# Gated cross-attention block: a tile's scores issued in two pieces, with a new plan of due times

## The chip, the core and the metric
The kernel runs on one core of a Trainium2 chip. The metric is device microseconds of one execution. Engines are written as the profile writes them: PE (TensorE matmuls), PEld (its weight loads), DVE (VectorE), ACT (ScalarE), POOL (GpSimd) and SP (SyncE, which issues the loads).

## What is computed
All is float32. For 8 batch entries of 256 tokens and width 128 there is first one gated cross-attention with 16 heads of 8, then six layers, each of windowed attention (16 heads of 64, windows of 32 queries that see their own and the previous window's 64 keys) and a gated feed-forward part.

```python
x = x + tanh(g_xattn) * xattn(layernorm(x), ctx, ctx)          # 16 heads of 8
y = layernorm(x)
for i in range(6):
    # attn: q, k, v = shift(y) @ Wqkv[i]; q, k are scaled to length 1, by q_scale, k_scale
    # and rotated; softmax(8 * q k^T) over 64 keys a window, masked; then @ v, then @ Wo[i]
    y = attn(shift(y)) + y
    # ffn: layernorm, a, gate = split(@ W1 + b1); (a * gelu(gate)) @ W2 + b2, inner width 341
    y = ffn(shift(y)) + y
out = x + tanh(g_ffn) * y
```

## The kernel before, in words
**Sequences and pieces.** Six layers of eight batch entries make 48 sequences, numbered k = layer * 8 + entry. A sequence's work is cut into small functions, the pieces. `at(k, piece, fn)` gives each piece the time k * 5 + PLAN[piece], in units of which a sequence has 5; all pieces of the program are then sorted by that time (the last lines of `tile_gated_block`, L928 to L930) and issued in that order. So PLAN alone sets the order in each engine's queue. PLAN spans 22 units, so that pieces of some four or five sequences are interleaved: "@-2" below means a piece of the sequence two before the current one. The framework adds the semaphore waits that the order needs. A tile is given to a new user once its last reader in program order has been issued; the new user waits for that reader.

**Pieces of a sequence** (t is one of two tiles of 128 tokens; each name with the line of its instruction):
- proj (L532, tile pj, PE): queries and keys, chunk c of 4 (k of tile 0, q of tile 0, k of tile 1, q of tile 1) in two halves. sq (L540, ACT) squares them into sq, which has one buffer; rot (L548, DVE) multiplies by the rotation tables; ss (L557, DVE) sums the squares; radd (L563, POOL) adds the halves of the rotation; norms (L571, ACT), ninv (L576 to L579, DVE) and nrm (L586, POOL) scale to length 1.
- pqt (L596, PE): 16 transposes of a chunk into the PSUM tile pqt; qe (L604, ACT): two copies of it into qT or kT.
- vp (L611, PE) and ve (L619, ACT): the values.
- sc0 and sc1 (L633, tile pss, PE): the scores of a tile, 8 pairs of heads * 2 * 4 windows, 64 calls, each of which is two weight loads and two matmuls of 64x64 in the profile, so 128 and 128.
- mx (L649, DVE): mask and maximum, group g = (tile, parity), half i: four heads (pairs 4i to 4i+3). ex (L659, ACT): exponentials and their sums of the same four. rs (L668, DVE) and div (L674, POOL): a group's division.
- pt (L692, tiles ppt, PE): 64 transposes of the probabilities of a tile; pe (L701 and L703, DVE, and ACT for (0, 0)) and co (L709, DVE) copy them to prT.
- at, aw (L730, tile po, PE) for two halves c: values by probabilities, with av (L741, DVE) between them and oe (L744, ACT) behind; wo (L753, PE) the output projection, oadd (L516 and L517, DVE).
- ftr (L766, tile px, PE) transposes back; fst (L182 to L185, DVE) the statistics; frs (L189, POOL) the power; fno (L193, tile xn, DVE); fba (L782, tile pxt, PE) transposes again; faf (L787, tile xnT, DVE); fga and fva (L802, tiles s and pa, PE) the up-projection, gate half first; fge (L809, ACT) gelu; fgt (L815, DVE); fdo (L826, tile pw, PE) the down-projection; fad.

**The cross stage**, one run for each batch entry (X0 to X7), begins ahead of the sequences: xt (L226) transposes, xqk (L234) projects, four units xs (L287, tile pssx, scores) with three maxima xm each (L297, DVE), xvp and xve (L252, L258) the values, xnt and xnc (L304 on PE, L308 on DVE, tile nm) turn the maxima, four units xp (L317, tile pssT) with exponentials xe (L328, ACT), xa and xo (L335, L343), then xu, xd, xw, xc, xwo (L348 to L378), xx, xst2, xr2, xn2, xt2, xsp (L381 to L401). Entry b's run is shifted by CROSS_SHIFT[b].

**PSUM.** Pool ps_p (2 buffers) holds pj, pv, px; ps_s (2 buffers of two banks) holds pqt, pss, po, one part of ppt, and s; ps_m (2 buffers) the others.

**Order of the issue of a sequence in the steady part**, from PLAN:

```
PE    proj01 fva@-4 proj00 at0@-3 sc1@-2 aw0@-3 fdo@-4 proj11 at1@-3 proj10 aw1@-3 pqt2@-1
      vp00@-1 wo0@-3 proj20 proj21 wo1@-3 pqt0@-1 pqt1@-1 proj31 ftr@-3 pt0@-2 sc0@-1 pqt3@-1
      vp10@-2 fba@-3 proj30 vp11@-1 fga@-3 pt1@-2 vp01@-2
DVE   ... rot20 rot21 oadd@-3 ss2 fst@-3 rot31 pe02@-2 fno@-3 mx01@-1 mx10@-1 pe01@-2 faf@-3
      rs2@-2 mx11@-1 mx00@-1 ss3 rot30 pe11@-2 pe12@-2 co@-2 pe10@-2
ACT   sq01 norms@-1 sq00 ex10@-2 oe0@-3 ex11@-2 sq11 ex00@-2 sq10 oe1@-3 ex31@-2 ve00@-1
      ex30@-2 sq20 qe21@-1 sq21 qe20@-1 ex20@-2 qe01@-1 qe00@-1 qe10@-1 qe11@-1 sq31 pe00@-2
      ex21@-2 qe31@-1 qe30@-1 ve10@-2 sq30 ex01@-1 ve11@-1 fge@-3 ve01@-2
```

**Order of a cross cycle** (X2 with X1 behind it and X0 ending):

```
PE    ... xa3.X1 xs2.X2 xa2.X1 xs1.X2 xu0.X1 xs0.X2 xu1.X1 xs3.X2 xt2.X0 xw.X1 xvp.X2 xnt.X2
      xt.X3 xp1.X2 xwo.X1 xqk.X3 xp0.X2 ...
```

Of the kernel before, what the change touches and what calls it, by code (L numbers as in the profile page):

```python
# [10 lines left out]
F32 = mybir.dt.float32  # L11
# [6 lines left out]
P = 128  # L18
# [7 lines left out]
DEPTH, HEADS, DH, WIN = 6, 16, 64, 32  # L26
KEYS = 2 * WIN
INNER = HEADS * DH
NPAIR = HEADS // 2
# [5 lines left out]


PLAN = {
    "proj01": 0.0, "sq01": 0.117, "rot01": 0.228, "proj00": 0.236, "sq00": 0.273, "rot00": 0.393,
    "ss0": 0.402, "proj11": 0.419, "sq11": 0.907, "rot11": 0.994, "proj10": 1.19, "sq10": 1.393,
    "rot10": 1.525, "ss1": 1.637, "radd1": 1.837, "proj20": 1.868, "sq20": 2.141, "rot20": 2.287,  # L40
    "proj21": 2.345, "sq21": 2.456, "rot21": 2.806, "ss2": 3.078, "radd0": 3.11, "proj31": 3.269,
    "sq31": 3.608, "rot31": 3.615, "proj30": 3.952, "sq30": 4.191, "radd2": 4.58, "ss3": 4.594,
    "rot30": 4.73, "norms": 5.141, "ninv": 5.35, "radd3": 5.599, "nrm2": 5.783, "nrm0": 5.955,
    "nrm3": 6.257, "pqt2": 6.415, "vp00": 6.565, "ve00": 6.664, "nrm1": 6.997, "qe21": 7.448,
    "qe20": 7.701, "pqt0": 7.799, "qe01": 7.896, "qe00": 7.932, "pqt1": 8.239, "qe10": 8.288,
    "qe11": 8.292, "sc0": 8.693, "pqt3": 8.78, "mx01": 8.907, "mx10": 8.927, "qe31": 9.004,
    "qe30": 9.09, "mx11": 9.28, "vp11": 9.287, "mx00": 9.458, "ex01": 9.514, "ve11": 9.589,
    "sc1": 10.324, "ex10": 10.374, "mx21": 10.605, "mx30": 10.609, "mx31": 10.696, "ex11": 10.807,
    "mx20": 10.859, "ex00": 11.32, "ex31": 11.408, "rs0": 11.679, "rs1": 11.757, "ex30": 11.855,
    "div1": 12.001, "rs3": 12.206, "div0": 12.294, "ex20": 12.875, "pt0": 13.461, "pe02": 13.622,  # L50
    "pe00": 13.707, "ex21": 13.784, "vp10": 13.787, "pe01": 14.102, "ve10": 14.121,
    "div3": 14.146, "rs2": 14.264, "div2": 14.336, "pt1": 14.54, "vp01": 14.624, "pe11": 14.821,
    "pe12": 14.867, "co": 14.868, "ve01": 14.935, "pe10": 14.949, "at0": 15.268, "av0": 15.27,
    "aw0": 15.36, "oe0": 15.434, "at1": 15.442, "av1": 15.705, "aw1": 16.363, "oe1": 16.404,
    "wo0": 16.588, "wo1": 17.415, "oadd": 17.94, "ftr": 18.346, "fst": 18.466, "frs": 18.529,
    "fno": 18.644, "fba": 18.801, "faf": 19.161, "fga": 19.492, "fge": 19.912, "fva": 20.011,
    "fgt": 20.187, "fdo": 20.398, "fad": 21.554, "zt": 21.653, "zg": 21.768,
    "xld": -22.25, "xst": -21.971, "xrs": -21.307, "xno": -20.581, "xt": -20.222, "xte": -20.092,
    "xqk": -19.736, "xqe": -19.735, "xke": -19.676, "xs2": -18.806, "xm21": -18.472,
    "xm22": -18.442, "xm20": -18.393, "xs1": -18.085, "xm11": -17.986, "xm12": -17.982,  # L60
    "xm10": -17.865, "xs0": -17.758, "xm01": -17.411, "xb": -17.355, "xm02": -17.348,
    "xs3": -17.326, "xm00": -17.273, "xm30": -17.198, "xvp": -17.075, "xm32": -17.038,
    "xm31": -17.012, "xve": -16.975, "xnt": -16.951, "xnc": -16.928, "xp1": -16.726,
    "xe12": -16.402, "xe11": -16.398, "xe10": -16.387, "xp0": -16.101, "xa1": -16.052,
    "xe02": -15.992, "xe01": -15.973, "xe00": -15.915, "xo1": -15.91, "xp3": -15.851,
    "xa0": -15.831, "xe31": -15.811, "xe32": -15.807, "xo0": -15.797, "xe30": -15.793,
    "xp2": -15.612, "xa3": -15.596, "xe21": -15.584, "xe22": -15.472, "xo3": -15.415,
    "xe20": -15.213, "xa2": -14.816, "xo2": -14.731, "xu0": -14.462, "xd0": -14.387,
    "xu1": -14.088, "xd1": -13.915, "xw": -13.791, "xc": -13.71, "xwo": -13.217, "xx": -13.195,
    "xst2": -12.619, "xr2": -11.475, "xn2": -10.599, "xt2": -10.456, "xsp": -10.398,  # L70
}

CROSS_SHIFT = [0.000, -1.653, -3.255, -4.780, -6.339, -7.886, -8.007, -9.173]
LOAD_FIRST, LOAD_AFTER, LOAD_AFTER_CROSS = -18.898, 21.60, -19.52

P_ON_SCALAR = {(0, 0)}

# [2 lines left out]
def tile_gated_block(ctx: ExitStack, tc: tile.TileContext, a: dict, out: bass.AP):  # L80
# [5 lines left out]
    small = ctx.enter_context(tc.tile_pool(name="small", bufs=4))  # L86
# [5 lines left out]
    ps_s = ctx.enter_context(tc.tile_pool(name="ps_s", bufs=2, space=PSUM))  # L92
# [10 lines left out]
    def at(k, piece, fn, *args):  # L103
        time = PLAN[piece] if isinstance(piece, str) else piece
        pieces.append((k * SLOTS + time, len(pieces), fn, args))

    def once(c_, key, pool, shape, tag, **kw):

        if key not in c_:
            c_[key] = pool.tile(shape, F32, tag=tag, name=tag, **kw)  # L110
        return c_[key]
# [86 lines left out]
    def cross(b):  # L198
# [203 lines left out]

        kx = b + CROSS_SHIFT[b] / SLOTS
        for n, fn in (
# [116 lines left out]
    def sequence(k, l, b, weights):  # L521

        c_ = {}
# [95 lines left out]
            nc.scalar.copy(v[:, t, half * 512 : (half + 1) * 512], c_.pop(("pv", t, half)))  # L619


        def scores(t):
            for x in ("sums", "rs"):
                c_[x, t] = small.tile([P, HEADS], F32, tag=x, name=x)
            pss = ps_s.tile([P, 2, NPAIR, KEYS], F32, tag="s", name="pss")
            c_["pss", t] = pss
            for c in range(NPAIR):
                for par in range(2):
                    rows = slice(par * DH, (par + 1) * DH)
                    for n in range(BLOCKS):  # L630
                        o = t * P + n * WIN
                        k0 = max(o - WIN, 0)
                        nc.tensor.matmul(  # L633
                            pss[n * WIN : (n + 1) * WIN, par, c, :],
                            c_["qT"][rows, c, o : o + WIN],
                            c_["kT"][rows, c, k0 : k0 + KEYS],
                            start=True, stop=True,
                        )
# [208 lines left out]
                at(k, f"vp{t}{half}", v_project, t, half)  # L847
                at(k, f"ve{t}{half}", v_evacuate, t, half)
        for t in range(NT):
            at(k, f"sc{t}", scores, t)  # L850
            at(k, f"pt{t}", p_transpose, t)
            for x in range(3):
                at(k, f"pe{t}{x}", p_evacuate, t, x)
# [67 lines left out]
    for l in range(DEPTH):  # L921
        at(l * B, tables, scale_tables, l)
        if l:

            at((l - 1) * B if l > 1 else B - 1, LOAD_AFTER if l > 1 else LOAD_AFTER_CROSS, load, l)
        for b in range(B):
            sequence(l * B + b, l, b, layers)
# [61 lines left out]
```

## Time and profile before
| what | value |
|---|---|
| median of three runs | 1841.89 us (1837.06 to 1842.74) |
| the profiled execution | 1843.98 us |
| its span, first to last instruction | 1842.2 us |
| mean granted TensorE clock | 0.974 |
| busy: PE, DVE, ACT, POOL | 1726.1, 1523.1, 1495.4, 1095.2 us |
| chain that ended last, by engine | PE 86%, DVE 6%, issue 5%, ACT 3%, POOL 1% |

A busy PE is a TensorE with matmuls in flight; the ends of matmuls are modelled, so times below are taken from one start to the next. The chain follows back from the last instruction what released each step; "issue" is time in which an engine waited for nothing that the profile shows. In the timeline, a row merges neighbouring instructions of a kind, and the bracket at its end is the engine's idle time ahead of it.

### The profile page before, as it was taken

To read this page: it belongs to the slowest core of one execution; us is meant where nothing else is said; L and a number is where in the kernel's file an instruction comes from. 1 tells how busy PE (TensorE), PEld (TensorE's weight loads), DVE (VectorE), ACT (ScalarE), POOL (GpSimd) and SP (SyncE) were. 2 spreads that over 40 slices of the span, in tenths; PEclk is the share of its full clock that TensorE was granted. 3 is DMA by queue.
4 is the path that set the end of the run, shared out by engine and by line. 5 is a ranking of instruction groups with operands and counts; after the bars stand their busy time and mean duration, and the time that the engine had idled before them with its cause. 6 is when DMAs were issued, how large, how long until landed. Compare 5 with 4: busy or idle time off the path is not lost.

```text
span 1842.2 us, 78203 instructions
## 1 busy us (share of the span) xinstructions
PE 1726.1 (94%) x32948; PEld 1151.3 (62%) x32948; DVE 1523.1 (83%) x5314; ACT 1495.4 (81%) x4692; POOL 1095.2 (59%) x716
## 2 busy tenths in 40 slices
PE   7999788999999999999999999999999999999987
PEld 4555454666666666666666666666666666666664
DVE  3544666888989999898999889999989999999864
ACT  2343357898989989898999989999989999998983
POOL 3111345665766667666676767767666777666741
PEclk9999989999999999999999999999999999999998
DMA  3000002000001000011000010000110000000000
GB/s 92 7 13 7 7 1 66 3 3 3 3 3 61 10 3 2 3 37 33 3 3 3 3 49 21 3 3 3 37 33 3 3 3 3 3 6 6 8 6 10
DMA packets 34717, 26.33 MB, mean 14 GB/s; under 512 B 16058, under 2 KB 31294, under 8 KB 34366
## 3 DMA queue, kind: packets, MB, share of 16 engines
q1 hardware_dynamic: 33214, 21.20, 3.9%
q8 instruction: 259, 4.24, 1.0%
q14 instruction: 92, 0.75, 0.1%
q10 hardware_dynamic: 1152, 0.14, 0.0%
HBM read 20.28 MB, written 1.05 MB: 12 GB/s over the span
## 4 chain that ended last, share of the span: by engine, by line
PE 86%; DVE 6%; issue 5%; ACT 3%; POOL 1%; POOLq 0%; ACTq 0%; DVEq 0%
PE pj L532 19%; PE pv L611 11%; PE m L753 9%; PE po L730 8%; PE pss L633 8%; PE pqt L596 6%; PE ppt L692 6%; PE s L802 5%; PE pssT L317 4%; PE pw L826 4%; DVE x_max L297 3%; PE pa L802 2%; PE pox L335 2%; ACT pr L328 1%; DVE ur L548 1%
## 5 line engine op out<-in xcount | busy, mean ns | idle before, releaser
L563 POOL TENSOR_TENSOR u<-ur 128x1024 f32<-128x1024 f32 x192 | 454.3, 2366 | 120.8 <-DVE ur L548 89.1
L659 ACT ACTIVATE pr<-pr,nmax 128x64 f32<-128x64 f32 x1536 | 515.2, 342 | 0.6
L586 POOL TENSOR_TENSOR u<-u,rn 128x1024 f32<-128x1024 f32 x192 | 361.3, 1903 | 192.0 <-DVE rn L579 192.0
L532 PE MATMUL pj<-w_qkv,st 128*128 128x512 f32 x768 | 404.4, 618 | 7.7 <-ACT x_big L343 2.3
L674 POOL TENSOR_TENSOR pr<-pr,rs 128x512 f32<-128x512 f32 x192 | 198.3, 1044 | 196.8 <-DVE rs L668 196.8
L659 ACT ACTIVATION_READ_ACCUMULATOR pr<-pr,nmax 128x1 f32 x1536 | 296.9, 193 | 0.0
L540 ACT ACTIVATE sq<-pj 128x512 f32<-128x512 f32 x384 | 230.3, 600 | 62.9 <-PE pj L532 52.2
L548 DVE TENSOR_TENSOR ur<-pj,rotk 128x1024 f32<-128x1024 f32 x192 | 227.1, 1202 | 44.9 <-ACT sq L540 43.8
L649 DVE CUSTOM_DVE_ANT_0 pr<-pss,mask 128x64 f32<-128x64 f32 x1536 | 233.6, 218 | 20.0 <-PE pss L633 19.4
L548 DVE TENSOR_TENSOR ur<-pj,rotq 128x1024 f32<-128x1024 f32 x192 | 230.1, 1218 | 14.0 <-ACT sq L540 13.8
L557 DVE TENSOR_REDUCE squares<-sq 128x16 f32<-128x1024 f32 x192 | 233.2, 1215 | 6.5 <-ACT sq L540 4.4
L611 PE MATMUL pv<-w_qkv,st 128*128 128x512 f32 x384 | 223.1, 664 | 0.8 <-DVE ur L548 0.8
L730 PEld LDWEIGHTS po<-prT,v 64*64 64x64 f32 x6144 | 134.3, 133 | 121.3 <-issue 38.7
L633 PE MATMUL pss<-kT,qT 64*32 64x64 f32 x12288 | 152.4, 227 | 46.8 <-issue 46.8
L532 PEld LDWEIGHTS pj<-w_qkv,st 128*128 128x128 f32 x768 | 134.7, 193 | 76.8 <-issue 38.8
L753 PEld LDWEIGHTS m<-oT,w_o 128*128 128x128 f32 x768 | 145.5, 190 | 58.9 <-issue 43.3
L753 PE MATMUL m<-oT,w_o 128*128 128x256 f32 x768 | 181.9, 380 | 0.0
L730 PE MATMUL po<-prT,v 64*64 64x96 f32 (+1 forms) x6144 | 171.5, 243 | 10.3 <-issue 6.2
L633 PEld LDWEIGHTS pss<-kT,qT 64*32 64x32 f32 x12288 | 130.5, 105 | 61.4 <-issue 53.4
L189 POOL TENSOR_TENSOR rstd<-rstd,half_neg 128x2 f32<-128x2 f32 x64 | 44.9, 702 | 176.0 <-DVE rstd L185 176.0
L604 ACT COPY qT<-pqt 128x512 f32<-128x512 f32 x192 | 104.3, 605 | 53.5 <-PE pqt L596 53.5
L701 DVE COPY prT<-ppt 128x512 f32<-128x512 f32 x192 | 127.3, 684 | 10.1 <-PE ppt L692 6.8
(116 smaller groups left out, 2879.0 us busy)
## 6 DMA issues: line engine op xcount, KB each, us to landing
w_qkv<-in_L_ffn_Wqkv SPq DMA_DIRECT2D x18, 512.0 KB, 5.6
w_o<-in_L_ffn_Wo SPq DMA_DIRECT2D x6, 512.0 KB, 4.1
w<-in_L_ffn_W SPq DMA_DIRECT2D x6, 341.0 KB, 2.8
xin<-in_x SPq DMA_DIRECT2D x8, 128.0 KB, 2.9
cin<-in_ctx SPq DMA_DIRECT2D x8, 128.0 KB, 2.1
out<-res SPq DMA_DIRECT2D x8, 128.0 KB, 1.8
w<-in_L_ffn_W SPq DMA_DIRECT2D x12, 64.0 KB, 3.4
rotq<-in_c_cos_q SPq DMA_DIRECT2D x6, 64.0 KB, 3.9
```

Of the source, the lines that this page charges most:

```text
L532: nc.tensor.matmul(pj, st[b][:, t * P : (t + 1) * P], w["qkv"][:, o : o + 512], start=True, stop=True,)
L540: nc.scalar.activation(sq[:, hs, :], c_["pj", c, half], AF.Square)
L548: nc.vector.tensor_tensor(ur[:, :, half * 512 : (half + 1) * 512].rearrange("p x (h d) -> p x h d", d=DH), pj.unsqueeze(1).to_broadcast([P ...
L557: nc.vector.tensor_reduce(squares[k % 2][:, t, i, :, 0], c_.pop(("sq", c)), AX.X, ALU.add)
L563: nc.gpsimd.tensor_tensor(u.rearrange("p h (two d) -> p h two d", two=2), ur[:, 0], ur[:, 1, :, ::-1, :], ALU.add,)
L586: nc.gpsimd.tensor_tensor(u, u, rn, ALU.mult)
L611: nc.tensor.matmul(pj, st[b][:, t * P : (t + 1) * P], w["qkv"][:, o : o + 512], start=True, stop=True,)
L633: nc.tensor.matmul(pss[n * WIN : (n + 1) * WIN, par, c, :], c_["qT"][rows, c, o : o + WIN], c_["kT"][rows, c, k0 : k0 + KEYS], start=True, ...
L649: nc.vector.tensor_tensor_reduce(probabilities(t)[:, par * NPAIR + c, :], c_["pss", t][:, par, c, :], mask[:, t, :], -1.0, 3e38, ALU.add, ...
L659: nc.scalar.activation(pr[:, col, :], pr[:, col, :], AF.Exp, bias=c_.pop(("nmax", g, c)), scale=-1.0, accum_out=c_["sums", t][:, col : col ...
L730: nc.tensor.matmul(po[par * DH : (par + 1) * DH, x, i, q0:q1], v[rows, t, h * DH : (h + 1) * DH], prT[rows, column[h], 64 * half : 64 * ha ...
L753: nc.tensor.matmul(pm, weights[l]["o"][:, c, :], oT[:, c, :], start=(first and c == 4 * half), stop=(not first and c == 4 * half + 3),)
```

## The change
`scores` takes a second argument: piece i issues the pairs 4i to 4i+3. Both pieces write the same PSUM tile, and the instructions are the same.

```diff
-        def scores(t):
+        def scores(t, i):
             for x in ("sums", "rs"):
-                c_[x, t] = small.tile([P, HEADS], F32, tag=x, name=x)
-            pss = ps_s.tile([P, 2, NPAIR, KEYS], F32, tag="s", name="pss")
-            c_["pss", t] = pss
-            for c in range(NPAIR):
+                once(c_, (x, t), small, [P, HEADS], x)
+            pss = once(c_, ("pss", t), ps_s, [P, 2, NPAIR, KEYS], "s")
+            for c in range(4 * i, 4 * i + 4):
...
         for t in range(NT):
-            at(k, f"sc{t}", scores, t)
+            for i in range(2):
+                at(k, f"sc{t}{i}", scores, t, i)
```

PLAN has a new time for every piece, CROSS_SHIFT and the times of the weight loads too:

```diff
-    "qe11": 8.292, "sc0": 8.693, "pqt3": 8.78, "mx01": 8.907, "mx10": 8.927, "qe31": 9.004,
+    "qe11": 7.79232, "qe10": 7.79416, "qe01": 7.86086, "qe00": 7.86486, "sc01": 8.08564,
+    "sc00": 8.08586, "mx01": 8.33529, "mx00": 8.575, "mx10": 8.73408, "ex01": 8.84437,
+    "mx11": 9.0029, "pqt3": 9.30081, "qe30": 9.30558, "vp11": 9.34495, "qe31": 9.3858,
...
-    "sc1": 10.324, "ex10": 10.374, "mx21": 10.605, "mx30": 10.609, "mx31": 10.696, "ex11": 10.807,
+    "ve11": 9.41571, "ex00": 10.61127, "sc10": 10.70937, "sc11": 10.76862, "mx20": 11.07451,
...
-CROSS_SHIFT = [0.000, -1.653, -3.255, -4.780, -6.339, -7.886, -8.007, -9.173]
-LOAD_FIRST, LOAD_AFTER, LOAD_AFTER_CROSS = -18.898, 21.60, -19.52
+CROSS_SHIFT = [0.0000000, -1.4843600, -2.9659400, -4.3950700, -5.7931900, -7.2641000, -8.5043100, -8.5733000]
+LOAD_FIRST, LOAD_AFTER, LOAD_AFTER_CROSS = -19.7106000, 21.63, -19.98
```

The order that follows from it, for the same stretches as above:

```
PE    proj01 fva@-4 proj00 at0@-3 sc10@-2 sc11@-2 aw0@-3 proj11 fdo@-4 at1@-3 proj10 aw1@-3
      pqt2@-1 vp00@-1 wo0@-3 proj21 proj20 wo1@-3 pqt1@-1 pqt0@-1 proj31 ftr@-3 pt0@-2
      sc01@-1 sc00@-1 vp10@-2 fba@-3 proj30 pqt3@-1 vp11@-1 fga@-3 pt1@-2 vp01@-2
DVE   ... rot21 rot20 oadd@-3 ss2 rs3@-2 fst@-3 rot31 pe01@-2 fno@-3 mx01@-1 mx00@-1 mx10@-1
      mx11@-1 faf@-3 rs2@-2 pe02@-2 rot30 co@-2 ss3 pe12@-2 pe11@-2 pe10@-2
ACT   norms@-1 sq01 sq00 ex00@-2 oe0@-3 sq11 ex10@-2 ex11@-2 sq10 oe1@-3 ve00@-1 ex30@-2
      qe21@-1 sq21 qe20@-1 sq20 ex31@-2 qe11@-1 qe10@-1 qe01@-1 qe00@-1 sq31 ex20@-2 pe00@-2
      ex21@-2 ve10@-2 ex01@-1 sq30 qe30@-1 qe31@-1 ve11@-1 fge@-3 ve01@-2
PE    ... xa3.X1 xt2.X0 xs2.X2 xa2.X1 xvp.X2 xs1.X2 xu0.X1 xs0.X2 xu1.X1 xs3.X2 xt.X3 xw.X1
      xwo.X1 xnt.X2 xp1.X2 xqk.X3 xp0.X2 ...
```

On DVE the cross cycle has xsp now ahead of the first maxima and xve behind the first three; on ACT xo3 now stands ahead of xe21; on POOL the bias sum of X0 and the clearing of tiles stand ahead of the norm of X1; nrm1 and radd2 come earlier.

## The prediction
> **What bounds the kernel now.** I read the page's busy shares first, then the waits, then TensorE's timeline in two sequences, then the busy time by stretch.
>
> ```profile
> span 1842.2 us, 78203 instructions
> PE 1726.1 (94%) x32948; PEld 1151.3 (62%) x32948; DVE 1523.1 (83%) x5314; ACT 1495.4 (81%) x4692; POOL 1095.2 (59%) x716
> ...
> q8 instruction: 259, 4.24, 1.0%
> ```
> TensorE is nearly full, and VectorE and ScalarE are close behind. The q8 line is the fetch of instructions: 4.24 MB over 32948 matmuls and as many weight loads is 64 bytes for one, and over 259 packets 16.4 KB, so one packet brings 256 instructions. 1.0% of 16 engines' span over 259 packets is about 1.14 us each.
>
> ```profile
> PEld pss L633 <- issue: 53.4, 38, 2.2
> PE pss L633 <- issue: 46.8, 37, 2.0
> ```
> These are the waits: TensorE stands still 46.8 us inside the scores, 37 times, and nothing that the profile shows holds it (the weight loads' row tells of the same time).
>
> ```profile
> 930.77 0.38 PE L766 MATMUL px<-ident,st 128*128 128x128 f32 x2
> 931.08 1.20 PE L692 MATMUL ppt<-ident,pr 32*64 32x32 f32 x64
> 932.21 1.07 PE L633 MATMUL pss<-kT,qT 64*32 64x64 f32 x84
> 934.18 0.68 PE L633 MATMUL pss<-kT,qT 64*32 64x64 f32 x44 [0.90 <-issue]
> ```
> ```profile
> 1497.33 0.38 PE L766 MATMUL px<-ident,st 128*128 128x128 f32 x2
> 1497.64 1.21 PE L692 MATMUL ppt<-ident,pr 32*64 32x32 f32 x64
> 1498.78 1.48 PE L633 MATMUL pss<-kT,qT 64*32 64x64 f32 x128
> ...
> 1501.80 0.38 PE L782 MATMUL pxt<-ident,xn 128*128 128x128 f32 x2
> ...
> 1503.73 1.46 PE L802 MATMUL s<-xnT,w 128*128 128x256 f32 x6
> ```
> TensorE's timeline (start, us, what) of two sequences of the same order: the first stops after 84 of 128 score matmuls, the second runs through. The stop is a block's end: in the trace's packets one of q8 starts at 931.65 us and lasts 1.33 us, and TensorE goes on 1.2 us after the packet. 64 transposes and 128 score matmuls are 384 instructions in 2.54 us (1497.64 to 1500.19), so a block of 256 that lies inside them is used up in 1.7 us, while packet and delay take about 3. One sequence later the stop comes after 83, because a sequence issues 638 pairs and 7 to 9 waiting instructions, some 1284, which is five blocks and four instructions. So the block's edge drifts about four instructions a sequence. From about 1350 us on it begins ahead of the run, among slow matmuls, and the stop is gone.
>
> ```profile
> 941.80:973.10 31.30, 30.38 (x640) 20.69 (x639) 29.22 (x106) 29.13 (x96) 21.68 (x14) 1.00 0.01 3
> 1447.00:1477.10 30.10, 30.10 (x639) 20.47 (x639) 28.83 (x106) 28.91 (x96) 21.62 (x14) 1.00 0.01 3
> 901.97:905.38 3.41, 3.41 (x28) 2.12 (x22) 1.85 (x17) 1.29 (x3) 0.00 (x0) 0.50 0.02 5
> ```
> Busy time by stretch (length, then PE, PEld, DVE, ACT, POOL, clock): a sequence with the stop takes 31.3 us, one without 30.1, and there TensorE is busy throughout, with VectorE and ScalarE only 1.2 us short of full. A long stop (1.69 us before 901.4) costs more: the next 3.41 us ran at a granted clock of 0.50.
>
> **The change, part by part.** *The scores in two pieces.* Both halves issue the same matmuls. In the new plan each pair stands directly together (3.08564 and 3.08586 in a period of 5; 0.70937 and 0.76862), with no TensorE piece between. Ahead of them stand, as before, the 64 transposes of pt0. Counting what each order issues ahead of pt0 gives the same number for every sequence from 1 to 47 (12 fewer for sequence 0), and I count the same seven waiting instructions, since PSUM slots go round in the same order. So the blocks fall where they fell: the stops stay, at 0 us of change. Bounds: a different count of waiting instructions by one a sequence moves the edge by a further 10 to 40 instructions over the kernel; stops then end earlier at the scores of tile 0 and begin earlier at those of tile 1 (128 of them between two dense attend pieces, where the trace has stops from 1637 us on), or the other way round: -10 to +10.
>
> [...]
>
> *TensorE's own pieces.* pqt3 goes behind fba and proj30, fdo behind proj11, pqt1 ahead of pqt0. By their start-to-start times in the clean sequence (0.64, 0.86 to 0.96, 1.40) the sequence stays at 30.1 us: 0.
>
> *VectorE's order ahead of the up-projection.* This is the term that I can see. Before, statistics, rot31, pe02, fno, mx01, mx10, pe01 and faf follow each other without a gap:
>
> ```profile
> 1500.62 0.72 DVE L193 TENSOR_SCALAR xn<-px,mv,rstd 128x128 f32<-128x128 f32 x2
> ...
> 1503.01 0.53 DVE L787 TENSOR_SCALAR xnT<-pxt,ln_g,ln_b 128x256 f32<-128x256 f32 x1
> ```
> TensorE starts fga at 1503.73, 0.19 us after xnT: no slack. In the new order all four maxima stand ahead of faf and only one copy. Two maxima pieces and the next start take 1.15 us (1501.26 to 1502.41), so four end at 1503.56, faf at 1504.09, and fga can start at 1504.28. TensorE would be there at 1497.33 plus 0.31 (ftr), 1.14 (pt0), 1.41 (scores), 0.96 (vp10), 0.22 (fba), 0.95 (proj30), 0.64 (pqt3), 0.86 (vp11), which is 1503.82. The wait is 0.46 us, and 0.66 if rs3, which moves ahead of the statistics, finds no idle time there; I take 0.6. Behind fga wait pt1 and all that follows on TensorE. pt1 also waits for qe31, which ScalarE now does behind ex01 and sq30 (by its queue about 0.6 us late); both waits overlap. In a sequence with a stop of 0.9 us or more TensorE comes later than xnT and the wait is covered. Left are the 13 sequences from 1350 us on: 13 x 0.6 = +8 us. Bounds 0 (VectorE ahead by its 1.2 us of spare time) and +13.
>
> *The cross stage (to about 185 us).* A cycle takes 31.0 us (xt at 93.26, 124.25) and is a chain: four score units on TensorE, their maxima on VectorE (112.22 to 123.77), xnt, the copy nm (124.34 to 124.77), xp1 (125.3). The plan takes xsp (0.85 us, at 120.47) out of the chain and puts xve (0.41) into it; xvp (0.54), now ahead of xs1, holds the next maxima up by some 0.35; xo3 (0.38) ahead of xe21 delays xs2 by 0.3. These cancel. But xwo (0.55), which stood behind xp1 on the chain, goes into the wait for the maxima: -0.55 a cycle, five cycles, -2.7. In the first cycle xt of sequence 1 no longer stands between xnt and xp1 (30.3 to 31.9) and the bias scaling (0.28) leaves the maxima: -2.3. Together -5. GpSimd's clear (25.4 to 29.4) moves ahead of xno of sequence 1, which then ends near 23, still in time. Bounds -10 and +5: TensorE ran at half clock in one window of nearly each cycle, and a window more or less is 1.7 us.
>
> *Cross and sequences mixed (185 to 330 us), and the end.* Here TensorE loses about 38 us (each piece's time from its start to the next piece's start in the timeline, less the usual one of that piece) to waits that change places in both orders; I can't follow them one by one. I take 0, the mean of the nearest rows' ends: -10 (a quarter of it) and +10. The loads on SP's queue keep their places (21.60 and 21.63). The last sequences lack the maxima of a successor: 0.
>
> **Sum.** The profiled execution took 1843.98 us (span 1842.2), 2.1 above the median of 1841.89. 1843.98 + 0 + 8 - 5 + 0 = 1847; against the median 1845.
>
> **Rivals.** *The stops go* (the plan does what it is said to do, by a count of instructions that I got wrong). For: they are the largest loss in the steady part. Against: 384 instructions still stand in a row. From 417 to 1346 us some 27 sequences would drop 1.15 us each and nine half-clock windows 1.7: -46, and the uncovered wait takes 27 x 0.6 back: 1815. [...] Chance 0.07.
> *The early part gains more*: the 97 us that TensorE loses up to 350 us (reckoned as the 38 above) shrink by a sixth, -16 in place of -5 (fewer half-clock windows, S0 begun earlier between X5's units): 1832. For: xsp, xwo and xt move into idle time; against: the chain over the maxima stays. Chance 0.21.
> *Slower: the cover fails.* ScalarE's sq11 now comes ahead of ex10 and must wait for ss0 (VectorE, 8.3 us into a sequence; ScalarE is there at 7.5), because sq has one buffer. If ScalarE doesn't make up these 0.8 us, sq21 and sq20 are late, then rot20, the statistics, xnT and fga: the wait is 1.4 us. It decides from where the slip passes 0.5 us, since then the wait passes the 1.15 us of the stop. 13 x 1.4 + 34 x 0.25 = 27 in place of 8: 1864; with half of the slip 1855. Against: ScalarE has 1.2 us to spare. Chance 0.31.
> *As forecast*, 1838 to 1852: 0.41.
>
> **The numbers.** I forecast 1845. The range 1826 to 1864 leaves out the first rival and the tails. About 0.3% is what a measurement of this kernel can tell from no change, so the bounds are 1836.4 and 1847.4. Faster: 0.07 + 0.19 + 0.02 = 0.28. Same: 0.28 of the forecast's 0.41, 0.02 each of the second and third = 0.32. Slower: the rest, 0.40.
>
> **What would show it.** Right: the scores (L633) stop in mid-run for "issue" as often as before, up to 1350 us; clean sequences take 30.6 to 30.8 us with a gap ahead of s (L802) or pxt (L782) put down to VectorE; xt of the cross stage comes every 30.4 us. Wrong: scores without stops, sequences of 30.1 us throughout, stalled sequences longer than 31.4, or a cycle of 29 us.

## The result and the profile after

| | before | after |
|---|---|---|
| median of the runs | 1841.89 us (5 runs, 1837.06 to 1845.77) | 1826.00 us (5 runs, 1818.11 to 1831.50) |
| ratio after/before | | 0.9919, 95% interval 0.9894 to 0.9943 |
| the profiled execution | 1843.98 us | 1818.11 us, the fastest of the five |
| mean granted TensorE clock | 0.974 | 0.988 |

The kernel is 16 us faster (10.5 to 19.5 by the interval); 1845 was forecast. The profiled executions are 25.9 us apart. The five runs of after differ with their mean clock (0.989 to 0.982), so the medians are the better measure of the size and the profiles of the place.

The page of after, its first lines, and from its waits the row of the scores:

```profile
span 1816.3 us, 78103 instructions
...
PE 1710.5 (94%) x32948; PEld 1136.4 (63%) x32948; DVE 1520.0 (84%) x5314; ACT 1496.5 (82%) x4692; POOL 1094.1 (60%) x716
```
```profile
PE s L637 <- issue: 44.5, 37, 1.8
```

The stops in the scores are still there: 37 as before, 44.5 us (before 46.8). The tile is called s here and the line is L637. So the split did not thin anything, as forecast. The busy time by stretch (length, then PE, PEld, DVE, ACT, POOL, clock) of a sequence without a stop and of one with it:

```profile
1479.40:1510.00 30.60, 30.58 (x639) 20.40 (x638) 28.81 (x106) 28.78 (x95) 22.12 (x14) 1.00 0.01 3
881.00:912.60 31.60, 30.41 (x639) 20.65 (x638) 28.97 (x106) 29.06 (x95) 21.52 (x14) 1.00 0.01 3
```

From start to start the undisturbed sequences take 30.69 us (before 30.10; the stretch is cut to a tenth), those with a stop 31.3 to 31.7 (before 31.1 to 31.5). The steady part has become no faster. Where the time went, by starts of pieces in the two traces, with the number of half-clock windows (granted clock 0.50 for 3.41 us) in each stretch:

| stretch | before | after | difference | half-clock windows |
|---|---|---|---|---|
| to xp1 of entry 5 (cross stage) | 192.1 | 179.5 | -12.6 | 6.0 and 0.2 |
| from there to sequence 5 (mixed) | 197.8 | 184.8 | -13.0 | 7.0 and 2.8 |
| sequences 5 to 35 (steady, with stops) | 966.9 | 959.8 | -7.1 | 11.0 and 6.0 |
| 35 to the last matmul | 482.0 | 488.8 | +6.8 | 4.0 and 3.0 |

The third row can be the clock's alone: a window at half clock loses at most 1.7 us (half of its 3.41), and five fewer are 8.5, an estimate. It is no gain of the new order, as the kernels below show. So the lasting gain lies ahead of sequence 5, half of it in the cross stage and half where cross stage and sequences are mixed. (Sequence 0 itself begins at 184.2 and 166.8 us, but its first projection is issued earlier among the units of entry 5: at xs2 of entry 5, ahead of it in both, the lead is 11.5 us.) TensorE's timeline (start, us, what) of the wait for the maxima in a cross cycle, before and after:

```profile
121.47 0.68 PE L252 MATMUL pv<-x_w,x_mid 128*128 128x128 f32 x4 [0.43 <-DVE st L401]
...
123.83 0.47 PE L304 MATMUL pn<-ident,x_max 128*128 128x128 f32 x1 [1.57 <-DVE x_max L297]
...
125.27 1.24 PE L317 MATMUL pssT<-x_big,xk 32*128 32x256 f32 x8
126.28 1.03 PE L317 MATMUL pssT<-nm,x_sel 32*128 32x256 f32 x8
```
```profile
115.63 0.41 PE L373 MATMUL pot<-ident,xo 128*128 128x128 f32 x2
116.59 0.71 PE L383 MATMUL pout<-x_w,oTt 128*128 128x128 f32 x4 [0.55 <-ACT oTt L377]
...
117.87 0.33 PE L309 MATMUL pn<-ident,x_max 128*128 128x128 f32 x1 [0.46 <-DVE x_max L302]
118.12 0.71 PE L322 MATMUL pssT<-x_big,xk 32*128 32x256 f32 x8
118.71 0.71 PE L322 MATMUL pssT<-nm,x_sel 32*128 32x256 f32 x8
```

Before, one wait of 1.57 us stands in front of the second transpose of xnt (pn), and the eight matmuls of xp1 (pssT) behind it take 1.24 us, at half clock. After, xwo (pout) lies inside the wait, the wait is two of about 0.5 us, and the same eight take 0.71. The cycle goes from 31.0 to 28.6 us; 30.4 was forecast.

VectorE's maxima of the same two cycles, the first and the last row of each, before and after:

```profile
112.22 2.42 DVE L297 TENSOR_REDUCE x_max<-pssx 128x2 f32<-128x512 f32 x3 [8.34 <-PE pssx L287]
...
121.36 2.42 DVE L297 TENSOR_REDUCE x_max<-pssx 128x4 f32<-128x1024 f32 x3
```
```profile
107.03 2.42 DVE L302 TENSOR_REDUCE x_max<-pssx 128x2 f32<-128x512 f32 x3 [1.38 <-PE pssx L292]
...
115.40 2.41 DVE L302 TENSOR_REDUCE x_max<-pssx 128x4 f32<-128x1024 f32 x3
```

### The profile page after: what moved, and what is told of

It reads as the page before. It is cut to its first block, busy times and chain, and to the rows that moved or that the text cites. A ratio compares the mean times of both kernels' runs of the same rounds, so it can differ in the third digit from the quotient of the medians.

```text
span 1816.3 us, 78103 instructions
## 1 busy us (share of the span) xinstructions
PE 1710.5 (94%) x32948; PEld 1136.4 (63%) x32948; DVE 1520.0 (84%) x5314; ACT 1496.5 (82%) x4692; POOL 1094.1 (60%) x716
## 4 chain that ended last, share of the span: by engine, by line
PE 83%; DVE 9%; issue 5%; ACT 3%; POOL 0%; POOLq 0%; DVEq 0%; ACTq 0%
PE pj L537 18%; PE pv L616 11%; PE m L757 8%; PE po L734 8%; PE s L637 7%; PE pqt L601 6%; PE ppt L696 5%; PE s L806 5%; PE pssT L322 4%; DVE x_max L302 3%; PE pw L830 3%; PE pa L806 2%; DVE ur L553 2%; PE pox L340 1%; PE pssx L292 1%
## 5 line engine op out<-in xcount | busy, mean ns | idle before, releaser
L653 DVE CUSTOM_DVE_ANT_0 pr<-s,mask 128x64 f32<-128x64 f32 x1536 | 232.6, 219 | 17.3 <-PE s L637 16.7
L637 PE MATMUL s<-kT,qT 64*32 64x64 f32 x12288 | 151.9, 226 | 44.5 <-issue 44.5
L624 ACT COPY v<-pv 128x512 f32<-128x512 f32 x192 | 112.7, 587 | 68.3 <-PE pv L616 68.2
L637 PEld LDWEIGHTS s<-kT,qT 64*32 64x32 f32 x12288 | 130.2, 105 | 58.7 <-issue 50.9
L601 PEld LDWEIGHTS pqt<-ident,u 64*128 64x128 f32 x3072 | 106.7, 139 | 60.2 <-ACT pr L663 28.8
```

The lines of the kernel that those rows point to most:

```text
L637: nc.tensor.matmul(pss[n * WIN : (n + 1) * WIN, par, c, :], c_["qT"][rows, c, o : o + WIN], c_["kT"][rows, c, k0 : k0 + KEYS], start=True, ...
L653: nc.vector.tensor_tensor_reduce(probabilities(t)[:, par * NPAIR + c, :], c_["pss", t][:, par, c, :], mask[:, t, :], -1.0, 3e38, ALU.add, ...
```

## The experiments

Each ratio is that of a kernel's runs to runs of the kernel before in the same batch. The stages are the stretches above, read from the profiled execution, with the half-clock windows of the second and third in brackets.

| kernel | ratio to before (95%) | cross | mixed | 5 to 35 | 35 to the end |
|---|---|---|---|---|---|
| before | 1 | 192.1 | 197.8 (7.0) | 966.9 (11) | 482.0 |
| after | 0.9919 (0.9894 to 0.9943) | 179.5 | 184.8 (2.8) | 959.8 (6) | 488.8 |
| cross_alone | 1.0125 (1.0104 to 1.0147) | 193.6 | 222.4 (13.8) | 952.9 (6) | 481.7 |
| cross_alone2 | 1.0097 (1.0069 to 1.0125) | 194.9 | 223.5 (12.3) | 946.7 (3) | 485.2 |
| cross_alone3 | 1.0069 (1.0043 to 1.0094) | 184.7 | 223.4 (12.2) | 955.7 (8) | 486.6 |
| seqs_alone | 1.0138 (1.0108 to 1.0168) | 188.5 | 217.9 (13.8) | 962.1 (8) | 491.0 |
| one_piece | 0.9907 (0.9880 to 0.9933) | 179.5 | 187.0 (4.8) | 958.7 (7) | 490.9 |
| undo_pe | 0.9950 (0.9926 to 0.9974) | 186.7 | 183.4 (1.0) | 960.2 (7) | 488.0 |
| undo_dve | 0.9988 (0.9965 to 1.0011) | 188.4 | 184.4 (2.0) | 957.6 (5) | 488.1 |
| hybrid | 0.9933 (0.9911 to 0.9956) | 177.3 | 183.9 (3.0) | 966.1 (7) | 482.6 |

**The parts of the plan.** First the new cross stage with the old sequences, and the reverse.

```diff
 # cross_alone: PLAN of before, with the times of all x pieces from after, and
-CROSS_SHIFT = [0.000, -1.653, -3.255, -4.780, -6.339, -7.886, -8.007, -9.173]
-LOAD_FIRST, LOAD_AFTER, LOAD_AFTER_CROSS = -18.898, 21.60, -19.52
+CROSS_SHIFT = [0.1, -1.38436, -2.86594, -4.29507, -5.71919, -7.1641, -8.40431, -8.2273]
+LOAD_FIRST, LOAD_AFTER, LOAD_AFTER_CROSS = -19.7106, 21.6, -19.98
```

> The kernel before (scores in one piece, the old order of the sequences) with the new times of the cross stage alone: all x pieces, the shifts of the entries and the first loads; the shifts are moved by at most 0.25 units, so that the two plans can be issued together. Theory A (the gain comes from the cross stage's new order): cycles of 28.6 us in place of 31.0, sequence 0 begins near 167 us (before 184.2, after 166.8), clean sequences still take 30.1 us, and the time is 1814 to 1826, below or at that of the kernel after (1826), since the 0.6 us of each clean sequence is not paid. Rival B (the new order of the sequences, or the split of the scores, makes it): sequence 0 near 184, time 1842 within 4.

Measured: cycles of 28.6 us, as theory A has it, but 1856.79 us. Sequence 0 began at 174.3: by the shift of 0.1 the load of the first weights had come ahead of the input of entry 1 on SP's queue, and xt of entry 1 came at 35.7 us (after: 27.9). And the mixed stretch took 222.4 us. (The shift of entry 7 differs from that of after by 0.35, more than the 0.25 stated.) Both theories were wrong in the time.

> The kernel before with the new times of the cross stage again (shifts moved as in the first run of this kind), but with the first load of weights moved by 0.09 units, so that it stands behind the input of entry 1 as in the kernel after; in the first run it stood ahead of it, and xt of entry 1 came 7.7 us late. Theory A: sequence 0 begins at 166.7 us, as in after: the 17.4 us up to there are the cross stage's alone. The stretch from sequence 0 to 3, where both are mixed, stays near 176 us (before 140, after 135), since it depends on how the two plans fit; time 1846 to 1852. Rival (the late input also made that stretch long): 145 us or less, time under 1822.

Measured: 1855.82 us, xt of entry 1 at 36.8. At -19.62 the load still stood ahead of the input (-19.6156), so this run only repeats the first.

> The same kernel once more, with the first load of weights at -19.60: at -19.62, in the second run of this kind, it still stood ahead of the input of entry 1 (at -19.6156), so that run told nothing new. Theory A: xt of entry 1 near 28 us (was 36), sequence 0 begins at 166.7 us as in after; sequences 0 to 3 still take 165 us or more (before 140, after 135), and the time is 1838 to 1852. Rival (the late input also made that stretch long): 145 us or less from sequence 0 to 3, time under 1822.

Measured: 1853.82 us; xt of entry 1 at 26.7, cycles of 28.6, sequence 0 at 164.7 us, 172.6 from there to sequence 3, xp1 of entry 4 at 144.6 us (before 156.1, after 146.7). So what the cycles gain is the cross stage's alone: it is there with the sequences and the scores of before. What it does not bring is the mixed stretch, 223.4 us. TensorE's longest waits from sequence 0 to 3, in this kernel (165 to 337 us) and in after (167 to 302 us):

```profile
PE pn L304 <- DVE x_max L297: 5.1, 3, 2.2
PE pox L335 <- ACT pr L328: 4.4, 2, 2.6
```
```profile
PE pj L537 <- DVE ur L553: 3.6, 4, 1.3
PE pssx L292 <- DVE x_max L302: 3.1, 1, 3.1
PE pox L340 <- ACT pr L333: 2.3, 4, 0.8
```

No single wait makes the difference. In all they are 46 us here and 21 in after; ten rows of the list have 2 us or more here, three in after. With them come half-clock windows: 12.2 in the mixed stretch, where after has 2.8. Which pieces don't fit each other isn't shown.

> The kernel after with the old times of the cross stage (shifts moved by 0.2 units): split scores and the new order of the sequences alone. Theory A: cross cycles of 31.0 us, sequence 0 near 184 us, clean sequences 30.7 us, so the time of before plus some 8 us: 1844 to 1854. Rival B: 1826 within 5.

```diff
 # seqs_alone: PLAN of after, with the times of all x pieces from before, and
+CROSS_SHIFT = [-0.2, -1.853, -3.455, -4.98, -6.539, -8.086, -8.207, -9.373]
+LOAD_FIRST, LOAD_AFTER, LOAD_AFTER_CROSS = -18.898, 21.63, -19.52
```

Measured: 1862.24 us; cycles of 31.0 to 31.5, sequence 0 at 186.5, 30.68 us for clean sequences, as theory A has it, and again a bad mixed stretch (217.9), which neither theory had. Over all kernels this stretch is 183 to 190 us with 1 to 5 half-clock windows in it, 197 to 198 with 7 to 8, and 218 to 224 with 12 to 14.

**The split alone.**

```diff
+PLAN.update({"sc00": 8.08564, "sc10": 10.76862})    # as sc01, as sc11
```

> The kernel after with the two pieces of a tile's scores at one time and in the order of before (pairs 0 to 7), for both tiles; all else as after. By theory A the split does nothing, since nothing is issued between the halves: the time of after, 1826 within 4, with as many stops in the scores (37, 44 us) and clean sequences of 30.7 us. Rival B (the halves let maxima or the copies behind them begin earlier): slower by 0.3 us or more in each of 47 sequences, 1838 or more.

Measured: 1816.92 us (before in this batch: 1836.69); the ratio is that of after (0.9907 and 0.9919). The split does nothing here, for good or ill.

**Which move in the cross cycle.** Two halves of the new cross order, each undone by itself in the cycles of the first entries.

```diff
+CYCLE = {"xt": -20.27, "xte": -20.26, "xwo": -13.0, "xx": -12.99}    # undo_pe, entries 0 to 4
+CYCLE = {"xno": -20.8, "xt2": -10.256, "xsp": -9.816}                # undo_dve, entries 0 to 3
...
-            at(kx, n, fn)
+            at(kx, CYCLE.get(n, n) if b < 5 else n, fn)    # 4 in undo_dve
```

> The kernel after, with one part of the new cross order undone for entries 0 to 4: xwo goes back behind xp1, and xt behind xnt (TensorE's order of before); VectorE's order stays new. Theory A1 (the gain per cross cycle comes from TensorE's pieces that now fill the wait for the maxima): the cycle goes from 28.6 to 29.2 us (xwo's 0.55 back on the chain), and to about 30.2 if TensorE's idle time ahead of xp1, then in one piece again, brings the half-clock windows back; time 3 to 8 us above after. Rival A2 (VectorE's chain of maxima alone sets the cycle): 28.6 and the time of after.

> The kernel after, with the other part undone for entries 0 to 3: xt2 and xsp (0.85 us on VectorE) go back among the maxima of the unit two entries later, and xno goes later, since its tile has one buffer; xwo and xt stay new. Theory A2: cycles of 29.4 us (28.6 + 0.85), time 3 us above after, more if half-clock windows come back. Theory A1: xsp fits into VectorE's idle time, 28.6 and the time of after.

Measured: cycles of 30.3 to 30.7 us in undo_pe, 30.3 to 31.7 in undo_dve. So neither theory holds alone: with either half undone nearly the whole gain of 2.4 us a cycle is gone (of the stage's 12.6 us, 7.2 and 8.9 are), and each is worth more than its own duration (0.55 and 0.85). In undo_pe the reason is the clock. Busy time by stretch, undo_pe first (the window in which xp1 runs, then the one ahead of it), then after at the same place:

```profile
61.71:65.12 3.41, 3.41 (x33) 2.46 (x29) 0.00 (x0) 0.43 (x2) 0.00 (x0) 0.50 0.00 0
...
58.29:61.71 3.42, 1.43 (x11) 1.02 (x15) 2.80 (x5) 0.56 (x2) 0.00 (x0) 1.00 0.00 0
```
```profile
61.71:65.12 3.41, 3.41 (x47) 2.65 (x47) 0.13 (x1) 1.91 (x4) 0.00 (x0) 1.00 0.27 77
...
58.29:61.71 3.42, 2.42 (x22) 1.44 (x24) 3.00 (x5) 0.86 (x2) 0.00 (x0) 1.00 0.00 0
```

In undo_pe TensorE is busy 1.43 of 3.42 us, and the next window runs at 0.50 and issues 33 matmuls; in after it is busy 2.42, and the next window runs at 1.00 and issues 47. xp1 takes 3.50 us there and 2.09 in after: 28.6 + 0.55 (xwo) + 1.41 = 30.6. In undo_pe the half-clock windows begin at 61.71, 92.43, 123.15 and 153.87, 30.72 us apart, which is nine windows of 3.413 (the half-clock ones are 3.41 long): with cycles of 30.3 to 30.7 us one falls on each xp1. In after's four cycles there is none. In undo_dve the clock is a part only. Half-clock windows fall on xp1 of entries 2 and 3 (2.75 and 3.73 us); but in the cycle before them, of 30.8 us, TensorE waits 1.5 us for the norm of a later entry (xno, on GpSimd), which this edit moves too. So how much of undo_dve's loss is that of xt2 and xsp alone isn't shown.

**Filling the wait with useless work.** If the low clock follows from the idle time, keeping TensorE busy in it should help though more is done.

```diff
 # before; x_max_transpose
+            for t in [0] * (10 if 1 <= b <= 4 else 0):
+                nc.tensor.transpose(pn[:, t, :], ident, ident)
```

> The kernel before, with useless work added: ten more transposes of 128x128 (some 1.4 us) into the tile pn ahead of xnt, for entries 1 to 4, in the 1.9 us in which TensorE waits for the maxima. Theory (the half-clock window at xp1 follows from TensorE's idle time just ahead of it): no half-clock window in these four cycles, xp1 takes 1.9 to 2.1 us in place of 2.8 to 3.7, and the cycle 30.0 us in place of 31.0, although more is issued. Rival (the lower clock has another cause, or follows from the idle time of the whole cycle): xp1 as before, cycles of 31.0 us or more.

TensorE's timeline of the same entry as above; L304 are the ten added transposes, L306 the two of xnt, L319 xp1:

```profile
119.40 0.98 PE L252 MATMUL pv<-x_w,x_mid 128*128 128x128 f32 x4 [0.43 <-DVE st L403]
120.17 2.34 PE L304 MATMUL pn<-ident 128*128 128x128 f32 x10
122.31 0.63 PE L306 MATMUL pn<-ident,x_max 128*128 128x128 f32 x2
...
123.42 0.71 PE L319 MATMUL pssT<-x_big,xk 32*128 32x256 f32 x8
123.96 0.61 PE L319 MATMUL pssT<-nm,x_sel 32*128 32x256 f32 x8
```

xp1 takes 1.94 us in place of 2.83, and from xt (92.68) to xt (122.73) it is 30.05 us in place of 31.0: as the theory said, by adding ten transposes a cycle. In all four entries xp1 takes 1.94 us (before 1.94, 2.97, 2.83 and 3.72). Two half-clock windows are still there: one at 41.1, where before has one too, and one at 119.64, which now falls on the useless work. Sequence 5 begins 7.2 us earlier than in before. The whole kernel is still no faster: 1844.12 us, ratio 1.0048 (1.0018 to 1.0078). The 40 transposes are 80 instructions, and they move all block edges by 80: at four a sequence, 20 sequences. The undisturbed sequences, 35 to 41 before, are now among 12 to 20 (those at 30.1 us), and from sequence 35 on there are two stops in most: 515.3 us from there to the end (before 482.0), which takes back what the middle gained (941.0, before 966.9).

**The forecast's 0.6 us in the clean sequences.**

```diff
+PLAN.update({"faf": 18.72})
```

> The kernel after with faf (time 18.72 in place of 19.0069) ahead of two of the four maxima (mx10, mx11). By the step of the forecast (four maxima ahead of faf make TensorE wait for xnT in clean sequences): clean sequences go from 30.7 to 30.1 or 30.2 us, stalled ones stay, time 4 to 8 us below after: 1818 to 1822. Rival (VectorE is nearly full, so the delayed maxima and copies make TensorE wait elsewhere): clean sequences stay at 30.6 or more, 1826 within 4.

Measured: 1825.35 us, ratio 0.9946 (0.9923 to 0.9970), not below after's 0.9919. The run tells nothing of the 0.6 us, since hardly a sequence was left without a stop. fga now has a waiting instruction of its own (L806: 46 in the trace, where after has 6), so by the count the edge drifts by five instructions a sequence and not by four; TensorE's waits put down to issue are 50, 59.5 us, where after has 44 and 52.1.

```diff
+OLD = {...}    # the times of before for all sequence pieces; sc00, sc01: 8.693; sc10, sc11: 10.324
-        time = PLAN[piece] if isinstance(piece, str) else piece
+        time = (OLD if k >= 6 and piece in OLD else PLAN)[piece] if isinstance(piece, str) else piece
```

> The kernel after, in which sequences from 6 on take the times of before (the halves of the scores at one time). If the gain is made up to sequence 5 (25.7 us ahead of before) and the new order of the sequences costs 0.6 us in each of some 13 clean sequences, as the forecast had it, this is the best of the three: clean sequences of 30.1 us, time 8 us below after, 1812 to 1819. Rival (the new order gains something in the steady part that the 0.6 us hide): 1826 or more.

Measured: 1826.31 us, the rival's number, with a ratio like that of after; the rival's reason doesn't show. Clean sequences take 30.1 us, and from sequence 35 to the end it is 482.6 us as in before: the step holds. But the seam costs what this saves: sequences 6, 7 and 8, where the two plans meet, take 39.8, 37.9 and 36.4 us.

**The split put to use.**

```diff
+PLAN.update({"fst": 17.955, "rot31": 2.952, "pe02": 13.225, "vp10": 13.08575, "fba": 18.34, "faf": 18.35})
+# thin01: also "fdo": 20.74
```

> The kernel after with the split put to use in tile 0: vp10 (two matmuls of 0.48 us) between the two halves of its scores; so that vp10 finds its buffer free, rot31 goes ahead of the statistics, and pe02, fba and faf go ahead of the later maxima. Theory (a stop is a block of 256 instructions that TensorE uses up faster than the next is fetched, about 3 us): a block that holds vp10 lasts 2.7 us in place of 1.7, so the stops of 1.2 us at the scores of tile 0 shrink to 0.3: 44 us of them to under 15, some half-clock windows go too, and the time is 1795 to 1812. Rival (the stops belong to the scores themselves, or the moved pieces make TensorE wait as long): 40 us or more of stops or of new waits, 1822 or more.

> As the kernel with vp10 between the halves of tile 0, and fdo (6 matmuls, 0.9 us) between the halves of tile 1's scores, where the last fifteen sequences stop. Theory: what is left of stops ahead of and in aw0 and at the second tile's scores (some 20 us) shrinks by half, 5 to 12 us below the kernel with vp10 alone. Rival: fdo there waits for the gate, or the moved edge finds other dense stretches: same within 4.

Measured: thin0 1849.65 us, ratio 1.0105 (1.0064 to 1.0146); thin01 1862.97 us, 1.0185 (1.0148 to 1.0223). The stops did go: from sequence 5 to 30 no wait of TensorE in thin0 is put down to issue (after has 25 in the scores between the same times, 30.6 us), and in the whole trace there are 17, 17.5 us. But each of these sequences takes 32.28 us. Its waits from 600 to 1200 us, 19 sequences:

```profile
PE pxt L786 <- DVE xn L198: 13.2, 19, 0.7
PE pv L616 <- DVE ur L553: 5.5, 19, 0.3
PE s L806 <- ACT qT L609: 3.8, 18, 0.3
```

By start to start vp10 comes 0.4 us late, fba 0.9 and fga 0.5, in all more than the 1.2 us of the stop. fdo in thin01 adds 0.5 us a sequence (32.79), which neither its theory nor its rival had. Two other orders, from sequence 2 on:

```diff
+# thin0c
+THIN = {"rot21": 2.3035, "rot20": 2.304, "proj31": 2.305, "sq31": 2.8, "rot31": 2.9412, "fst": 17.942, "vp10": 13.08575, "pqt3": 8.6, "fba": 18.61, "faf": 18.62}
+# thin0d
+THIN = {"proj31": 3.0857, "pqt3": 8.6, "sq31": 3.5987, "rot31": 3.5988, "fba": 18.605, "vp10": 13.607, "mx00": 8.62, "faf": 18.63}
```

> The kernel after; for sequences from 2 on, vp10 again between the halves of tile 0's scores, but with VectorE's order chosen so that little waits: pe02 stays late, sq31 goes ahead of qe01 and qe00, rot31 ahead of the statistics, pqt3 ahead of fba, faf behind two maxima. In the kernel with vp10 moved first (32.28 us a sequence) the stops had gone but TensorE waited 0.29 us for rot31, 0.71 for xn and 0.21 for xnT. Theory (these waits came from pe02 ahead of fno and from rot31's wait for sq31, not from the split): 30.4 to 30.9 us a sequence up to sequence 30 and no stop in the scores there, time 1790 to 1806. Rival (VectorE and ScalarE are too full for any such order; the wait only moves): 31.5 us or more, 1822 or more.

> The same with another filler: for sequences from 2 on, proj31 (two matmuls) between the halves, with sq31 and rot31 behind it, ftr earlier by its 0.96 us, vp10 behind fba. Theory: sc01 waits 0.3 us for the copies of kT, otherwise nothing: 30.4 to 30.9 us a sequence, time 1790 to 1806. Rival: 31.5 us or more, 1822 or more.

Measured: thin0c 1869.89 us, ratio 1.0184 (1.0125 to 1.0243), 32.75 us a sequence; thin0d 1857.06 us, 1.0112 (1.0059 to 1.0164), mostly 31.6 to 32.7. Both are the rival's case. The waits of thin0c in the same 600 us:

```profile
PE s L806 <- ACT qT L609: 24.1, 18, 1.4
PE s L637 <- ACT kT L609: 7.4, 18, 0.4
```

fga now waits 1.4 us for the copies of pqt3, whose buffer it takes. thin0d still has a stop of some 0.5 us in the scores in 12 of these 19 sequences, though two matmuls of half a microsecond stand between the halves there too, and waits of 0.2 to 0.3. What thin0 has besides is the wait of 0.29 us ahead of vp10, inside the same block. Where the rest of thin0d's 1.5 us lies I can't say.

## Why the prediction was wrong

*The cross stage: the step that failed.* The term was -5, bounds -10 and +5; measured is -12.6. Two parts of it failed. The first: "The plan takes xsp (0.85 us, at 120.47) out of the chain and puts xve (0.41) into it; xvp (0.54), now ahead of xs1, holds the next maxima up by some 0.35; xo3 (0.38) ahead of xe21 delays xs2 by 0.3. These cancel." They don't: VectorE's chain from the first maxima to the last went from 11.55 us (112.22 to 123.77) to 10.78 (107.03 to 117.81), 0.77 a cycle. xwo's 0.55 was right. The second stood in the bounds and not in the sum: "TensorE ran at half clock in one window of nearly each cycle, and a window more or less is 1.7 us". I took these windows for chance. They go with the idle time that the change fills, so they had to be in the sum: in before TensorE was busy for 1.33, 1.52 and 1.61 of the 3.41 us ahead of the three windows at 93.00, 123.72 and 154.44, and after has none in these cycles. xp1 of entries 2 to 4 took 2.83 to 3.72 us where 2.09 is now enough, 0.7 to 1.6 a cycle, 3.2 in the three. The cycles bear both out. From xp1 to xp1, that of entry 1, whose xp1 ran at full clock before too (1.94 us), went from 29.96 to 28.61, which is 0.77 + 0.55; the next two lost 2.4 and 2.25. There 0.77 + 0.55 and 0.9 or 0.7 for xp1 make 2.2 and 2.1; the rest isn't followed. The kernels with one half undone, and the one with useless transposes, show the part of the clock; the one with the cross stage alone shows that the sequences' plan has none in it.

*Cross and sequences mixed, 0 with -10 to +10:* measured -13.0, also outside. Here too the windows were a missing term: four fewer, at 1.7 us each, are an estimated 7 us at most. Which moves make the rest I can't say; the joined plans show only that the stretch depends on how the two parts fit.

*Scores, 0:* right. 37 stops as before, and one_piece is as fast.

*VectorE's order, +8:* right in mechanism for the clean sequences, near in size partly by luck. They cost 0.59 us more (0.6 reckoned), and fga starts 0.06 us after xnT ends, at the end of a chain in which VectorE has had no gap since the statistics:

```profile
1505.85 0.54 DVE L791 TENSOR_SCALAR xnT<-pxt,ln_g,ln_b 128x256 f32<-128x256 f32 x1
1506.45 1.56 PE L806 MATMUL s<-xnT,w 128*128 128x256 f32 x6
```

The list of waits doesn't have this one, since the modelled end of the matmuls ahead covers it; by start to start a part of it (0.18 us) lies ahead of fba already, which needs xn. From sequence 35 to the end the profiles with the new order take 488.0 to 491.0 us (after, one_piece, seqs_alone, undo_pe, undo_dve), those with the old one 481.7 to 486.6 (before, the three of the cross stage alone, hybrid): 5.7 us between the means. All of it lies in sequences 35 to 41, which take 210.6 to 213.1 us with the old order and 216.6 to 218.8 with the new. So seven sequences were clean before, not 13, and each lost more than 0.6, since some of them stop again. The second half of the step failed: that a stop covers the wait, so that stalled sequences pay nothing. Where no half-clock window falls on them, the stalled ones up to sequence 33 take 31.3 to 31.4 us in the median with the old order (five kernels) and 31.4 to 31.6 with the new (five): some 0.13 us more each, which over the thirty sequences of the middle is an estimated 4 us.

*Rivals.* The second, that the early part gains more by fewer half-clock windows and an earlier sequence 0 (-16), is what happened, 1832 by its price, 1826 by the median. It had 0.21, because I held the chain over the maxima for fixed. ScalarE's slip (0.31) doesn't show in the clean sequences, which lost 0.59 us and not 1.4; its other term, 0.25 us in a stalled sequence, is not far from the 0.1 to 0.2 measured, but no run shows that ScalarE is the cause. The stops did not go (0.07).

*What also moved:* the steady middle, -7.1 in the profile, with five half-clock windows fewer. That is the luck of the two profiled executions: before's has 11 windows there, the others with the old order 2 to 8, and at the same number of windows the new order is the slower one (959.8 and 952.9 us with 6, 962.1 and 955.7 with 8). With -12.6 and -13.0 ahead of sequence 5, an estimated 4 us lost in the middle and the 5.7 at the end, the sum is -16, close to the difference of the medians.

## What to carry to other kernels

Where TensorE waits in a chain, look at how long it is busy in a clock window of 3.41 us and at the clock of the next (undo_pe: 1.43 us, then 0.50; after: 2.42, then 1.00). Two edits that each fill part of a wait paid little or nothing alone and more than their sum together (cycles of 31.0 us before, 30.3 to 30.7 and 30.3 to 31.7 with one, 28.6 with both), and filling a wait, even with useless work, kept the clock up in the work behind it (xp1 1.94 us in place of 2.83). A plan of due times is a matched whole: either half of the better one, joined to the old other half, was slower than both. Stops for instruction fetch can be scheduled away (17 waits put down to issue in place of 44), but here, with TensorE at 94%, VectorE at 84% and ScalarE at 82%, the waits that took their place cost more (32.28 us a sequence in thin0, where a sequence with a stop takes 31.3 to 31.7). Instructions added to TensorE's queue move the later stops: 80 in fill_gap moved the undisturbed sequences by some 20.

## What the runs showed of the hardware

The clock: in after, the windows followed by a half-clock one, themselves at full clock, had TensorE busy for 2.2 of 3.41 us or less, and those followed by a full one for 1.76 or more (from 60 us on, by the modelled ends). So the two overlap near 2 us, and busy time alone doesn't tell them apart: windows with 2.42 us in before (at 226.13) and with 2.50 and 2.95 in fill_gap (at 116.22 and 218.62) were followed by a half-clock one too. What else counts isn't shown.

The fetch: in before and after, TensorE goes on at each of the 37 stops 2.2 to 2.9 us after the start, and 1.1 to 1.6 after the end, of a packet of queue q8 (instruction), 16,384 bytes, which at the forecast's 64 bytes for one is a block of 256 instructions; so the forecast's 3 for packet and delay is high. How long a stop is went with how long the block lasts. Blocks that are used up in an estimated 1.7 us (256 of the 384 instructions that take 2.54) stop TensorE for about 1.2 (44.5 us in 37 stops of after). With two matmuls of about 0.5 us more inside the block (thin0d) the stops are some 0.5 us (6.1 us in 12 sequences of 19) or gone; with two such and a wait of 0.29 (thin0) they are gone from sequence 5 to 30. Block and stop together come to some 3 us each time, an estimate from these numbers. In fill_gap 80 added instructions moved the undisturbed sequences by some 20, which is the drift of four a sequence that the forecast had read from the trace of before.
